# Cumulative sums of the cascade's next segment, issued two interleaving steps later

## The chip, the cores and the metric

The kernel runs on one core of a Trainium2 chip. The metric is the device time of one execution in microseconds (us). Three runs of the kernel before gave 21643.39, 21647.89 and 21668.76 us; the median is 21647.89 us. The engines are called PE (TensorE, matmuls), DVE (VectorE), ACT (ScalarE), POOL (GpSimd) and SP (the queue that issues all DMAs here).

## What is computed

The reference is a network of two layers on x of shape 8 x 128 x 64 x 64. Each layer adds a token mixer and a feed-forward part. The change touches only one part of the second layer's mixer, the *cascade*: two blocks of a Mamba-2 kind in a row, on eight groups of 16 channels, over sequences of 4096 tokens, for each of the 8 images. Cut to what matters, one block is

```
zxbcdt = x @ in_w.T + in_b                     # z, x, B, C, dt
dt  = softplus(dt + dt_bias);  A = -exp(A_log)
xBC = silu(conv3(x, B, C) + conv_b)
Acs  = cumsum(dt * A) within a chunk           # the cumulative sums
Lmat = exp(Acs[l] - Acs[s]) for l >= s
Yd = (C . B) * Lmat @ (x * dt)                 # inside a chunk
states = B * exp(Acs[-1] - Acs) * (x * dt)     # what a chunk adds to the state
Yo = C . state_before * exp(Acs)               # from earlier chunks
y  = (Yd + Yo + D * x) * silu(z);  y = rmsnorm(y) @ out_w.T
```

The state goes from chunk to chunk, so the chunks of one block and one image form a chain. The second block reads the first block's output.

## The kernel before

The 4096 tokens of an image are cut in segments of 256 tokens, 128 segments in all, and each segment in two chunks of 128. Three generators make a segment, and a hand-written loop interleaves them. Each `yield` ends a step.

`ssd_project` (line 942) prepares a segment. It yields after each of two groups of `bc_p` matmuls with their Silu, after `z_p`, after the first `tok_p`, and "silu" after the second `tok_p`, where the activation table for Exp and Ln is loaded (line 321). Its next step (lines 999 to 1007) is softplus: Abs, Exp and Ln on ACT and five small DVE operations, which end in `dA = dt * A`. The next step (line 1008) is `ssd_exponents` (line 914): the matmul `cs_p` makes the cumulative sums of dA, four DVE operations (lines 926 to 929) split them into three bf16 parts `csq`, one DMA writes these to DRAM (line 931), and 16 DMAs load them back as rows (`ssB`, line 936, four; `ssA`, line 939, twelve). The next step (lines 1011 to 1023) makes `dec_p` and its Exp `wd`, multiplied by dt on DVE, and `cd_p` and its Exp `cd`. The last one (lines 1025 to 1034) makes `eA` from the parts with twelve bf16 matmuls. After it, block 0 issues the loads for its next segment (line 1364).

`ssd_chunk` (line 1036) computes one chunk in seven steps:
1. `g_p` (C . B) and its masked copy `gm`; `pad` and `xw` on DVE (x times dt, x times wd); `xD` on POOL.
2. `decays(0)`: four `ss_p` matmuls from `ssA` and `ssB`, and two Exps `E`.
3. `yo_p` from the old state copy `Sd`; `s_p` from `xw`; `masked(0)` (the two E times gm, DVE); the new state `S`, and its copies `Sd` on POOL.
4. `decays(1)`, and the mark "decays".
5. `inside(0)`: `y_p`, the product of E and pad; `yy`; `masked(1)`.
6. `inside(1)`.
7. `yy` plus `y_p`, times silu(z).

`ssd_output` (line 1151) normalizes a segment and projects it with `o_p`.

PSUM has two pools of tiles in the cascade. Tag "a" has two tiles of two banks (`bc_p`, `z_p`, `tok_p`, `g_p`, `ss_p`, `eA_p`, `ms_p`), tag "b" four tiles of one bank (`cs_p`, `dec_p`, `cd_p`, `yo_p`, `s_p`, `y_p`, `o_p`).

The loop at lines 1432 to 1455 takes, for each n, the chunks x[0] (block 0, segment n, first chunk), x[1] (block 1, segment n - 2, first chunk), x[2] (block 0, second chunk) and x[3] (block 1, second chunk). `until(gen, mark, others)` advances gen step by step up to the mark, and after each of its steps advances the first of the others that is not finished by one call. The segment n + 1 of block 0 is prepared beside x[0] up to "silu"; from there the generator is wrapped in `slow`, which gives an empty step ahead of each step's own yield, so that each step takes two calls: the first call after "silu" runs softplus, then come two calls beside the rest of x[1], then four beside x[2] up to "decays", and then `drain` runs all that is left. The segment n - 1 of block 1 is treated in the same way after x[2], beside x[3] and the next x[0]. So `ssd_project` comes twice in a pass of the loop, 256 times in all.

The order of instructions on each engine is not exactly that of the code: Tile orders them when the program is made, from what is ready and from the order in which the code issued them, and gives out the PSUM tiles. Each engine then runs its own list in order, and waits on semaphores. `self.mm`, `self.act`, `self.tt` and the like are helpers, so most instructions of the profile carry the line of a helper (L287, L290, L329, L338) and are told apart by their tiles.

Of the kernel before, what the change touches and what calls it, by code (L numbers as in the profile page):

```python
# [278 lines left out]
class Net:  # L279
# [1054 lines left out]
    def cascade(self, ps):  # L1334

        nc, tc = self.nc, self.tc
        total = self.nb * NSC
        with tc.tile_pool(name="cs", bufs=1) as pl, tc.tile_pool(name="csw", bufs=2) as wk:  # L1340
            ring = self.ssd_rings(pl, CM, SC, 3, 3, 4)
            st = [{"ring": ring, "S": None, "layer": j} for j in range(2)]
            stk, y1, seg = {}, {}, {}

            def place(n):
                return n // NSC, n % NSC

            def load(layer, n):
                if not 0 <= n < total:
                    return  # L1350
                b, k = place(n)
                src = self.xs[b] if layer == 0 else y1[b]
                stk[layer, n] = self.tap_stack(src, k * SC, k == 0, ring)

            def project(layer, n):
                if not 0 <= n < total:
                    return
                t = stk.pop((layer, n))
                for v in self.ssd_project(CM, self.ssw[layer], ring, lambda j: t[:, j, :], SC, wk, ps):
                    if isinstance(v, dict):  # L1360
                        seg[layer, n] = v
                    yield v
                if layer == 0:
                    load(0, n + 1)

            def chunk(layer, n, c):
                if not 0 <= n < total:
                    return
                if c == 0 and n % NSC == 0:
                    st[layer]["S"] = None  # L1370
                yield from self.ssd_chunk(CM, self.ssw[layer], st[layer], seg[layer, n], c, wk, ps)

            def output(layer, n):
                if not 0 <= n < total:
                    return
                b, k = place(n)
                sg = slice(k * SC, (k + 1) * SC)
                for o in self.ssd_output(CM, self.ssw[layer], seg.pop((layer, n)), SC, wk, ps):
                    if o is None:
                        yield  # L1380
                if layer == 0:
                    if k == 0:
                        y1[b] = self.dp.tile([C, L], F32, name="y1", bufs=2)
                    y = wk.tile([C, SC], F32, name="y1s")
                    nc.scalar.copy(y, o)
                    nc.sync.dma_start(y1[b][:, sg], y)
                    load(1, n)
                else:
                    x = wk.tile([C, SC], F32, name="ys")
                    nc.sync.dma_start(x, self.xs[b][:, sg])  # L1390
                    self.stt(x, x, self.w("skip"), o, ALU.mult, ALU.add)
                    nc.vector.tensor_reduce(self.gms[:, b, k : k + 1], x, AX.X, ALU.add)
                    nc.sync.dma_start(self.ys[b][:, sg], x)

            def until(gen, mark, others=()):

                for v in gen:
                    for o in others:
                        if next(o, self) is not self:
                            break  # L1400
                    if v == mark:
                        break

            def between(gen, then):

                yield from gen
                yield next(then, None)

            def both(*gens):

                gens = list(gens)
                while gens:
                    for g in list(gens):
                        if next(g, self) is self:
                            gens.remove(g)
                        yield None

            def drain(*gens):
                for g in gens:
                    for _ in g:  # L1420
                        pass

            def slow(gen):

                for v in gen:
                    yield None
                    yield v

            load(0, 0)
            drain(project(0, 0))  # L1430
            late = p = iter(())
            for n in range(total + 2):
                x = [chunk(0, n, 0), chunk(1, n - 2, 0), chunk(0, n, 1), chunk(1, n - 2, 1)]
                until(x[0], "decays", [p])
                drain(p)
                p = project(0, n + 1)
                rest = between(x[0], x[1])
                until(p, "silu", [rest])
                drain(rest)
                until(x[1], "decays", [late])  # L1440
                p = slow(p)
                next(p, None)
                until(x[1], "end", [p])
                until(x[2], "decays", [p])
                drain(p, late)
                p = project(1, n - 1)
                rest = between(x[2], x[3])
                until(p, "silu", [rest])
                drain(rest)
                first = slow(output(0, n))  # L1450
                until(x[3], "decays", [first])
                p = slow(p)
                next(p, None)
                until(x[3], "end", [p, first])
                late = both(first, slow(output(1, n - 2)))
            drain(late)
# [254 lines left out]
```

## Time and profile before

| What | Value |
|---|---|
| Median of three runs | 21647.89 us |
| The profiled execution | 21652.28 us |
| Its span, first to last instruction | 21650.5 us |
| Mean granted PE clock | 0.930 |
| PE busy | 17287.7 us, 80% |
| DVE busy | 15953.5 us, 74% |
| ACT busy | 11620.6 us, 54% |
| POOL busy | 8896.4 us, 41% |
| `cs_p` of the cascade, first and last start | 11382.2 and 19813.8 us |

A row of the waits view reads: engine and what it was about to run, what it waited for, us in total, times, longest. A row of the timeline reads: start in us, duration in us, engine, line, operation, output <- inputs, shapes, number of instructions merged; in brackets the engine's idle time before it and what ended that. One float32 matmul of the code stands as two instructions, one bf16 matmul as one. Records of a few matmuls can be missing. A row of the windows view gives the busy time of each engine in a stretch, with the number of instructions.

### The profile page before, as it was taken

What the parts mean: (1) busy time and instruction counts of PE and PEld (TensorE: products, weight loads), DVE (VectorE), ACT (ScalarE), POOL (GpSimd) and SP (SyncE); (2) the same over time, 40 slices, a digit from 0 to 9 for tenths busy, and PEclk for the clock granted to TensorE, in tenths of its full rate; (3) what the DMA queues carried; (4) which work ended last, traced back from release to release, by engine and by line L of the source; (5) the groups of instructions that cost most, each with busy time, mean ns of one, the idle gap of its engine ahead of it and who ended that gap; (6) DMA issues with size and microseconds to landing.
All of it is one profiled execution on the core that took longest, in us unless ns stands there. A gap on an engine that the chain in (4) does not pass through costs nothing. (4 is left out here: it accounts for less than half of the span.)

```text
span 21650.5 us, 300665 instructions
## 1 busy us (share of the span) xinstructions
PE 17287.7 (80%) x112733; PEld 8832.8 (41%) x112733; DVE 15953.5 (74%) x21079; ACT 11620.6 (54%) x17646; POOL 8896.4 (41%) x6004
## 2 busy tenths in 40 slices
PE   6777777777777777777778888888888888887999
PEld 2222222222222222225345555555555555554343
DVE  7979798897979889794555666666666666666887
ACT  6555555555555555552535555555555555555442
POOL 6757576675757677573111111111111111112221
PEclk9989899998999999997778999999999999998999
DMA  4534344443434444344420000000000000001110
GB/s 113 130 103 131 103 131 120 115 129 106 129 106 130 111 123 130 106 130 118 137 88 21 25 24 24 24 25 24 24 24 25 24 24 24 24 25 33 39 41 25
DMA packets 804462, 1616.84 MB, mean 75 GB/s; under 512 B 179579, under 2 KB 411931, under 8 KB 802267
## 3 DMA queue, kind: packets, MB, share of 16 engines
q1 hardware_dynamic: 803006, 1597.61, 26.9%
q8 instruction: 891, 14.60, 0.3%
q14 instruction: 565, 4.63, 0.1%
HBM read 1373.56 MB, written 223.74 MB: 74 GB/s over the span
## 5 line engine op out<-in xcount | busy, mean ns | idle before, releaser
L287 PE MATMUL dA<-parts,expand 128*128 128x512 bf16 x12288 | 3448.3, 390 | 2441.5 <-ACT dA L290 1768.8
L329 POOL TENSOR_TENSOR bx<-xE,B 128x1024 f32<-128x1024 f32 x2048 | 4822.2, 2357 | 753.3 <-DVE dA L621 406.9
L290 ACT ACTIVATE dA<-dA,negA 128x512 f32<-128x512 f32 x4096 | 2709.4, 661 | 3726.9 <-PE dA L287 3704.3
L621 DVE TENSOR_TENSOR_SCAN dA<-dA,last,bx 128x1024 f32<-128x1024 f32 x1536 | 3612.2, 2352 | 177.5 <-ACT dA L290 156.7
L287 PEld LDWEIGHTS <-expand 128*128 128x128 bf16 x12288 | 1197.0, 98 | 5226.6 <-issue 4514.1
L338 DVE SCALAR_TENSOR_TENSOR E_cm<-E_cm,gm_cm 128x1024 f32<-128x1024 f32 x2048 | 2444.7, 1235 | 295.0 <-ACT E_cm L290 279.5
L329 DVE TENSOR_TENSOR hc<-dA,C 128x1024 f32<-128x1024 f32 x2048 | 2508.2, 1225 | 166.7 <-DVE dA L621 3.2
L290 ACT ACTIVATE E_cm<-ss_p 128x1024 f32<-128x1024 f32 x2048 | 1998.0, 1023 | 1139.4 <-PE ss_p L287 1134.3
L1129 POOL COPY Sd_cm<-S_cm 64x128 f32<-64x128 f32 x1024 | 785.4, 767 | 3812.3 <-DVE S_cm L329 3699.3
L287 PE MATMUL ss_p<-ssB_cm,ssA_cm 128*128 128x512 bf16 x4096 | 1327.1, 408 | 494.4 <-ACT E_cm L290 407.8
L287 PE MATMUL y_p<-E_cm,pad_cm 128*32 128x128 f32 x32768 | 1457.4, 285 | 47.0 <-DVE E_cm L338 47.0
L621 DVE TENSOR_TENSOR_SCAN dA<-dA,bx 128x1024 f32<-128x1024 f32 x512 | 1174.0, 2293 | 188.5 <-POOL bx L329 128.1
L329 POOL TENSOR_TENSOR xD_cm<-tok_cm,D_cm 128x256 f32<-128x256 f32 x512 | 433.6, 847 | 2001.3 <-PE y_p L287 1206.0
L287 PE MATMUL y<-hc,kt 128*32 128x512 f32 x8192 | 1199.0, 652 | 26.1 <-DVE hc L329 26.1
L287 PEld LDWEIGHTS y_p<-E_cm,pad_cm 128*32 128x32 f32 x32768 | 944.7, 112 | 429.3 <-DVE E_cm L338 158.8
L287 PE MATMUL bc_p<-stk_cm,W_cm 128*128 128x256 f32 x4096 | 1014.4, 391 | 23.9 <-DMA stk_cm<-xs 20.7
L290 ACT ACTIVATE tok_cm<-tok_p 128x384 f32<-128x384 f32 x1024 | 502.9, 491 | 702.7 <-PE tok_p L287 608.6
L329 DVE TENSOR_TENSOR gm_cm<-g_p,kt 128x1024 f32<-128x1024 f32 x512 | 626.0, 1223 | 333.5 <-PE g_p L287 333.3
L338 DVE SCALAR_TENSOR_TENSOR dw<-h,w_second,dw 128x512 f32<-128x512 f32 x1024 | 858.3, 863 | 5.5 <-ACT h L290 1.0
L290 ACT ACTIVATE BC_cm<-bc_p 128x1024 f32<-128x1024 f32 x512 | 524.4, 1024 | 608.7 <-PE bc_p L287 607.2
L287 PE MATMUL tok_p<-W_cm,stk_cm 128*128 128x200 f32 x4096 | 828.2, 345 | 0.1
L287 PEld LDWEIGHTS bc_p<-stk_cm,W_cm 128*128 128x128 f32 x4096 | 750.3, 191 | 189.5 <-issue 94.6
(387 smaller groups left out, 30583.2 us busy)
## 6 DMA issues: line engine op xcount, KB each, us to landing
xE<-dtx_d SPq DMA_DIRECT2D x2048, 512.0 KB
dtx_d<-dtx SPq DMA_DIRECT2D x256, 256.0 KB
x<-x SPq DMA_DIRECT2D x192, 256.0 KB
ssA_cm<-cs_cm SPq DMA_DIRECT2D x3072, 4.0 KB
stk_cm<-xs SPq DMA_DIRECT2D x368, 128.0 KB
stk_cm<-y SPq DMA_DIRECT2D x368, 128.0 KB
x<-in_x_dram SPq DMA_DIRECT2D x64, 256.0 KB
x<-r SPq DMA_DIRECT2D x64, 256.0 KB
```

The lines of the kernel that those rows point to most:

```text
L287: self.ordered(self.nc.tensor.matmul(out, lhsT=lhsT, rhs=rhs, start=start, stop=stop))
L290: i = self.ordered(self.nc.scalar.activation(out, in_, func, **kw))
L329: self.ordered((eng or self.nc.vector).tensor_tensor(out, a, b, op))
L338: self.ordered(self.nc.vector.scalar_tensor_tensor(out=out, in0=a, scalar=s, in1=b, op0=op0, op1=op1))
L621: self.ordered(nc.vector.tensor_tensor_scan(out=t, data0=t, data1=bx.pop(n), initial=0.0 if ch["j"] == 0 else last[:, q : q + 1], op0=ALU. ...
L1129: nc.gpsimd.tensor_copy(Sd[gr, :, g * hi : (g + 1) * hi], S2[gr])
```

## The change

`slow` gets a second argument. The first value of the wrapped generator is preceded by `more` further empty steps; the later ones by one, as before. Both preparations are wrapped with `more = 2`, the outputs as before.

```diff
-            def slow(gen):
+            def slow(gen, more=0):
 
                 for v in gen:
-                    yield None
+                    for _ in range(1 + more):
+                        yield None
+                    more = 0
                     yield v
...
                 until(x[1], "decays", [late])
-                p = slow(p)
+                p = slow(p, 2)
                 next(p, None)
                 until(x[1], "end", [p])
                 until(x[2], "decays", [p])
...
                 until(x[3], "decays", [first])
-                p = slow(p)
+                p = slow(p, 2)
                 next(p, None)
                 until(x[3], "end", [p, first])
```

Softplus is still run by the first call. `ssd_exponents` is run by call 5 in place of 3, the step of dec and cd by call 7 in place of 5, that of eA by call 9 in place of 7, and the loads by call 11 in place of 9. Calls from 8 on are made by the drain.

## The prediction

> **What bounds the kernel now.** I read the page first: the change touches only the cascade, which lies between about 11,400 and 19,840 us, and there TensorE (PE) is the fullest engine. The windows view gives it 7356 of these 8440 us, VectorE (DVE) 5254, ScalarE (ACT) 4721. Then the waits of PE in that stretch, then the timeline at its two largest holes.
>
> ```profile
> engine line waited for: us in total, times, longest us
> PE cs_p L287 <- DVE dA_cm L329: 408.2, 248, 3.8
> PE ss_p L287 <- ACT E_cm L290: 407.1, 508, 1.5
> ...
> PE ss_p L287 <- DMA ssB_cm<-cs_cm: 13.6, 4, 7.6
> ```
>
> So the matmul of the cumulative sums waits for dA, which softplus has just made; the loads of the cs rows make PE wait for almost nothing. One pass of the loop takes 65.0 us (cs_p comes at 14022.33 and again at 14087.28), and 128 segments pass. 408.2 / 128 = 3.19 us of wait per pass. It falls in two places. After layer 1's first chunk (place A):
>
> ```profile
> 14018.21 0.49 PE L287 MATMUL y_p<-kt,xD_cm 128*128 128x128 f32 x2
> 14018.53 0.59 PE L287 MATMUL ss_p<-ssB_cm,ssA_cm 128*128 128x512 bf16 x2
> 14019.51 0.38 PE L287 MATMUL ss_p<-ssB_cm,ssA_cm 128*128 128x512 bf16 x1 [0.38 <-DVE dtr_cm L989]
> 14022.33 0.43 PE L287 MATMUL cs_p<-kt,dA_cm 128*64 128x128 f32 x2 [2.44 <-DVE dA_cm L329]
> 14022.69 0.43 PE L287 MATMUL dec_p<-dA_cm,kt 128*128 128x64 f32 x2
> 14023.06 0.34 PE L287 MATMUL cd_p<-dA_cm,kt 128*64 128x32 f32 x4
> 14023.33 1.03 PE L287 MATMUL ss_p<-ssB_cm,ssA_cm 128*128 128x512 bf16 x2
> 14024.30 1.12 PE L287 MATMUL yo_p<-BC_cm,Sd_cm 128*64 128x128 f32 x6
> ```
>
> and after layer 1's second chunk (place B):
>
> ```profile
> 14063.38 0.43 PE L287 MATMUL cs_p<-kt,dA_cm 128*64 128x128 f32 x2 [0.90 <-DVE dA_cm L329]
> 14063.74 0.93 PE L287 MATMUL g_p<-BC_cm 64*128 64x128 f32 x10
> 14064.60 0.60 PE L287 MATMUL ss_p<-ssB_cm,ssA_cm 128*128 128x512 bf16 x2
> 14065.04 0.33 PE L287 MATMUL dec_p<-dA_cm,kt 128*128 128x64 f32 x2
> 14065.31 0.31 PE L287 MATMUL cd_p<-dA_cm,kt 128*64 128x32 f32 x4
> 14065.44 0.64 PE L287 MATMUL yo_p<-BC_cm,Sd_cm 128*64 128x128 f32 x8
> ```
>
> A waits 2.44 us, B 3.19 - 2.44 = 0.75 on average. After A the windows view shows a further cost (columns: stretch, its us, busy PE, PEld, DVE, ACT, POOL, granted clock, DMA share, GB/s):
>
> ```profile
> 14018.60:14022.30 3.70, 0.91 (x4) 0.13 (x2) 2.06 (x9) 3.53 (x7) 0.50 (x2) 1.00 0.47 145
> 14022.30:14026.80 4.50, 4.47 (x31) 2.53 (x31) 2.36 (x7) 1.23 (x3) 0.00 (x0) 0.62 0.25 67
> 14063.40:14067.50 4.10, 4.10 (x48) 2.97 (x49) 4.03 (x11) 2.38 (x5) 0.00 (x0) 1.00 0.00 2
> ```
>
> PE is busy 0.91 of 3.70 us, and then runs at a mean granted clock of 0.62 for 4.5 us; after B, with the short wait, it stays at 1.00.
>
> **The change part by part.** Counting the calls of the slowed generator: softplus stays at call 1; cumulative sums move from call 3 to 5, dec/cd from 5 to 7, eA from 7 to 9, the next load from 9 to 11. Two calls fall in the old chunk's rest, four in the next chunk up to "decays", the rest in the drain. So cs_p, its four casts and its 17 DMAs are now issued after the next chunk's g_p, gm, pad, xw, xD and first four ss_p; dec_p, cd_p, wd and cd after its yo_p, s_p, first masks, state update, Sd copies and last ss_p. eA and the load are issued directly behind them, past nothing else. Nothing is added or removed, and the softplus chain (table load 1.28 us, then ACT and DVE up to dA) is untouched: what can change is only what PE does while it runs.
>
> Place B. PE now reaches g_p (0.93) and two ss_p (0.60) ahead of cs_p; they ran straight after it without a wait, so they were ready. Together they are longer than the 0.90 us hole: saved 0.75 us per pass. Bounds: 0, if g_p were ready only because cs_p took the time, and 0.90.
>
> Place A. Here the next chunk's g_p cannot fill the hole, since it needs one of the two double banks that ss_p and its Exp hold. But yo_p and s_p of that chunk can. Their operands are old (the state copy Sd ended at 14007.02, xw at 14018.56 at the latest), and yo_p still ran only at 14024.30, about 0.9 us after the Exps that empty dec_p and cd_p at 14023.38 and 14023.64. I read that as a matter of banks: cs_p, dec_p, cd_p, yo_p, s_p and y_p share four single banks and take them in the order in which the code issues them, and y_p holds one. So cs_p, dec_p and cd_p hold the other three while they wait for dA. With dec_p and cd_p issued behind yo_p and s_p, the two get the banks at about 14018.7 and fit in the hole. What that is worth: yo_p 0.64 us (x8, place B) and s_p 0.80 us (16 of them, windows view restricted to s_p, 14063.40 to 14067.90) make 1.44 us of PE work moved out of the path behind cs_p. Bounds: 0, if the banks are not the reason, and 2.44 + 0.38 (the dtr wait before it) if ss_p too fills what is left.
>
> The clock. At 0.62 over 4.5 us PE loses (1 - 0.62) x 4.5 = 1.71 us per pass. If the hole shrinks from 2.44 to 1.0 us, this may go or stay; B's row, at 1.00 after 0.90 us of wait, is the nearer one, A's is the other end. Bounds 0 and 1.71; I take half, 0.85.
>
> The Trainium skill ("TensorE: Matmul & The Clock Gate", HAM oscillation) says that only idle gaps of more than some 3.4 us bring the clock down. A's 2.44 us gap, with 0.62 after it, contradicts that here. By the page this term would be nothing and the time 109 us longer than mine.
>
> What the moves cost. PE: cs, dec, cd are 0.43 + 0.33 + 0.31 us wherever they stand. DVE: the four casts (0.28, 0.28, 0.21, 0.27) fall behind gm (1.23); at B gm already runs between the second and third cast, so the last ends at most 0.5 us later. wd is next read by xw some 5.1 us after it is made at 14001.72 (xw at 14006.79); moving dec_p past yo_p, s_p and two ss_p (0.64 + 0.80 + 0.60) stays inside that cover, and beyond it each us would be a us of xw. SP issues 17 DMAs, the write at 14001.82, the last at 14012.8; the write took 2.70 us to be followed by the first load, so the last rows are there by about 14015.5 (an estimate). Layer 1's ss_p reads them from 14018.53: 3.0 us of cover, against a delay I put at 0.5 to 1.5 us. For A's sums the same reader comes 40 us later. POOL: xD and Sd now stand ahead in issue, but nothing in the moved chain runs there. No wait is added.
>
> What is late next: at A, dA itself at 14022.28. PE gets 1.44 us of work and waits for the rest. Behind it the stretch 14038 to 14053 is PE busy 14.18 of 14.80 us, and 14067.5 to 14083.6 wholly busy, so what PE gains is passed on.
>
> Sum: 1.44 + 0.75 + 0.85 = 3.04 us per pass, x 128 = 389 us. The profiled execution took 21652.28 us (span 21650.5), 4.4 us above the median of 21647.89, so the two can be used alike: 21652 - 389 = **21,263, say 21,260 us**. Without the clock 21,372; with all upper bounds (2.82 + 0.90 + 1.71 = 5.43 us) 20,957.
>
> **The rivals.**
> 1. Only B changes. cs_p at A still goes first because nothing else gets a bank. For it: the order at A held in every pass I looked at. Against: the operands of yo_p were ready. Price: 0.75 x 128 = 96 us, 21,556.
> 2. It does nothing. The order on each engine is set when the program is made, ready work first, and a later issue need not move an instruction that is ready alone; or B's 0.75 is given back as Exp waits of ss_p, which already cost 407.1 / 128 = 3.18 us per pass. 21,650, within 43 us.
> 3. Slower: the rows come late. The sums of B feed, through 17 DMAs, layer 1's ss_p one chunk later. It decides when the casts fall behind more than gm: behind the four masks as well (1.21 each, 4.84) the rows come 1.23 + 4.84 - 3.0 = 3.1 us too late, or the program is ordered so that ss_p stands behind yo_p, cs_p, dec_p and cd_p for the same reason. Less B's 0.75 and A's 1.44 that is 0.9 us, and without A's gain 2.3: 115 to 294 us, middle 205, so 21,857. Against it: the casts are still issued before those masks, and only 13.6 us of waits on these loads are seen now.
>
> **How the numbers follow.** Forecast 0.55 (21,000 to 21,430), rival 1 0.18 (21,430 to 21,605), rival 2 0.11, rival 3 0.16. Forecast and rival 1 are faster by over 0.2% (43 us, about what a measurement of this kernel can tell from no change): 0.73 faster, 0.11 same, 0.16 slower. The range runs from 21,000 (just above the sum of upper bounds, which I give 0.03) to 21,700, so that most of rival 3 and that tail, under 0.2, are left out.
>
> **What would show it.** In the changed trace: at A, yo_p and s_p of the next chunk stand before cs_p, its wait is about 1 us, the clock after it nearer 1.00; at B, g_p and ss_p stand before cs_p and its wait is gone; the passes are 62 us apart. Wrong if cs_p still waits 2.4 us at A (rival 1 or 2), if ss_p at A comes behind cs_p, or waits for ssB or ssA rows by more than 0.5 us per pass (rival 3).

## The result, and the profile after

The changed kernel takes 21954.59 us (median of four runs, 21926.02 to 21963.47), the kernel before 21649.85 us beside it (21643.39 to 21668.76). The ratio is 1.0137, with an interval of 1.0122 to 1.0152: **305 us slower**, where 21,260 us had been forecast. The profiled execution took 21963.47 us, with a span of 21961.5 us and a mean granted clock of 0.911 in place of 0.930.

First, where the time lies. From the first to the last `cs_p` the cascade takes 8728.4 us in place of 8431.6, which is 68.19 in place of 65.87 us for each of 128 passes. These 297 us are nearly the whole difference, which is 311 us between the spans of the two profiled executions (21961.5 and 21650.5). The windows view over the whole cascade (stretch, its us, then busy us of PE, PEld, DVE, ACT and POOL with the number of instructions, clock, DMA share, GB/s), before and then after:

```profile
11400.00:19840.00 8440.00, 7356.18 (x76461) 4992.77 (x76460) 5253.75 (x10174) 4720.63 (x6760) 1534.05 (x1785) 0.95 0.08 24
```

```profile
11400.00:20140.00 8740.00, 7570.53 (x76407) 5152.40 (x76410) 5146.97 (x10168) 4720.56 (x6761) 1150.01 (x1782) 0.90 0.08 23
```

The same work, 76 thousand matmuls, keeps PE busy 214 us longer, while DVE and ACT are not busy longer. PE's idle time grows by only 300 - 214 = 86 us. So most of the loss is not waiting. The matmuls themselves have become longer, and the mean granted clock, 0.90 in place of 0.95, points to the cause.

Now the waits of PE in that stretch (engine and what it was about to run, what it waited for, us in total, times, longest):

```profile
engine line waited for: us in total, times, longest us
PE ss_p L287 <- ACT E_cm L290: 479.7, 647, 1.5
PE cs_p L287 <- DVE dA_cm L329: 437.3, 129, 3.8
...
PE ss_p L287 <- DVE gm_cm L329: 76.3, 104, 0.8
...
PE ss_p L287 <- DMA ssB_cm<-cs_cm: 19.8, 5, 7.5
```

`cs_p` waits about half as often, 129 times in place of 248, but longer in sum, 437 us. The wait at place B is gone and that at place A has grown. PE waits for the rows of `ssB` and `ssA` for 19.8 us in the whole cascade. They are not late for the hole at A either: the last three of their DMAs are issued in the 1.12 us from 14046.30 on, and between 14049 and 14054 no DMA moves anything, while `y_p`, the last matmul ahead of the hole, runs at 14051.44 (windows view: stretch, its us, busy us of PE, PEld, DVE, ACT and POOL, clock, DMA share, GB/s):

```profile
14046.30 1.12 SPq L939 DMA_DIRECT2D ssA_cm<-cs_cm  x3
14049.00:14054.00 5.00, 2.93 (x35) 2.11 (x33) 2.23 (x10) 3.59 (x8) 0.81 (x2) 1.00 0.00 0
```

The timeline of the changed kernel at A:

```profile
14051.44 0.49 PE L287 MATMUL y_p<-kt,xD_cm 128*128 128x128 f32 x2
14055.28 0.44 PE L287 MATMUL cs_p<-kt,dA_cm 128*64 128x128 f32 x1 [3.36 <-DVE dA_cm L329]
...
14055.68 0.90 PE L287 MATMUL yo_p<-BC_cm,Sd_cm 128*64 128x128 f32 x6
...
14056.40 1.20 PE L287 MATMUL s_p<-xw_cm,tok_cm 128*64 128x32 f32 x13
14057.52 1.46 PE L287 MATMUL ss_p<-ssB_cm,ssA_cm 128*128 128x512 bf16 x3
```

Between `y_p` and `cs_p` there is now nothing. The three `ss_p` of x1 that stood there before are behind `cs_p`, `yo_p` and `s_p`, and the hole is 3.36 us in one piece, where it was 0.38 + 2.44. `yo_p` and `s_p` have not moved ahead of `cs_p`. At B the prediction's picture is there, at a small price, a wait of `ss_p` for gm:

```profile
14099.35 0.93 PE L287 MATMUL g_p<-BC_cm 64*128 64x128 f32 x10
14100.21 0.60 PE L287 MATMUL ss_p<-ssB_cm,ssA_cm 128*128 128x512 bf16 x2
14100.75 0.32 PE L287 MATMUL cs_p<-kt,dA_cm 128*64 128x128 f32 x1
...
14102.79 0.59 PE L287 MATMUL ss_p<-ssB_cm,ssA_cm 128*128 128x512 bf16 x2 [0.74 <-DVE gm_cm L329]
```

Last, the clock. The trace records when the granted clock changes (start in us, length in us, share of full speed). Around place A, in the kernel before and then in the changed one:

```
before  14023.192   3.413  0.5        after  14054.374  13.653  0.5
        14026.605  61.440  1.0               14068.027  54.613  1.0
```

All these lengths are multiples of 3.413 us. The clock thus goes by windows of that length, and the useful view is one that cuts the time at their edges. Before, at A:

```profile
14019.78:14023.19 3.41, 0.97 (x9) 0.62 (x8) 1.45 (x7) 2.40 (x6) 0.00 (x0) 1.00 0.71 206
14023.19:14026.60 3.41, 3.41 (x24) 1.75 (x24) 1.81 (x5) 1.01 (x3) 0.00 (x0) 0.50 0.07 17
14026.60:14030.02 3.42, 2.87 (x50) 1.80 (x47) 2.86 (x4) 2.35 (x3) 2.05 (x2) 1.00 0.18 52
```

and after:

```profile
14050.96:14054.37 3.41, 0.97 (x8) 0.39 (x4) 2.04 (x11) 2.91 (x6) 0.81 (x2) 1.00 0.03 12
14054.37:14057.79 3.42, 2.51 (x25) 2.33 (x26) 2.03 (x8) 0.00 (x0) 0.00 (x0) 0.50 0.08 28
14057.79:14061.20 3.41, 3.41 (x14) 1.52 (x12) 1.82 (x4) 1.45 (x3) 1.43 (x2) 0.50 0.37 110
14061.20:14064.61 3.41, 2.87 (x16) 1.02 (x18) 2.34 (x4) 2.68 (x3) 0.26 (x1) 0.50 0.34 70
14064.61:14068.03 3.42, 3.42 (x38) 2.32 (x39) 1.69 (x2) 0.28 (x1) 0.72 (x1) 0.50 0.08 17
14068.03:14071.44 3.41, 2.45 (x42) 1.61 (x41) 1.87 (x3) 0.92 (x1) 0.00 (x0) 1.00 0.27 85
```

In both kernels a window in which PE is busy 0.97 of 3.41 us is followed by one at half speed. Before, that one is busy throughout, and the clock is back after it. After, the hole reaches over the edge of the window and takes 0.91 us of the next one too (`cs_p` comes at 14055.28); later `ss_p` waits 0.54 us for E, and the clock is back only after four windows. PE is at half speed for 1734.5 us of the cascade in place of 884.7, which is 13.55 us per pass in place of 6.91.

### The profile page after: what moved, and what is told of

It is laid out like the page before. It is cut to its first block, busy times and chain, and to the rows that moved or that the text cites. A ratio compares the mean times of both kernels' runs of the same rounds, so it can differ in the third digit from the quotient of the medians.

```text
span 21961.5 us, 300764 instructions
## 1 busy us (share of the span) xinstructions
PE 17517.6 (80%) x112733; PEld 8999.6 (41%) x112733; DVE 15850.8 (72%) x21079; ACT 11623.6 (53%) x17646; POOL 8519.6 (39%) x6004
## 5 line engine op out<-in xcount | busy, mean ns | idle before, releaser
L287 PE MATMUL ss_p<-ssB_cm,ssA_cm 128*128 128x512 bf16 x4096 | 1387.4, 437 | 584.9 <-ACT E_cm L290 479.7
L1129 POOL COPY Sd_cm<-S_cm 64x128 f32<-64x128 f32 x1024 | 457.8, 447 | 3565.4 <-DVE S_cm L329 3456.6
L287 PE MATMUL y_p<-E_cm,pad_cm 128*32 128x128 f32 x32768 | 1575.2, 300 | 4.3 <-DVE E_cm L338 4.2
L329 POOL TENSOR_TENSOR xD_cm<-tok_cm,D_cm 128x256 f32<-128x256 f32 x512 | 379.2, 741 | 2825.8 <-PE y_p L287 2177.8
L287 PEld LDWEIGHTS y_p<-E_cm,pad_cm 128*32 128x32 f32 x32768 | 1004.6, 118 | 496.3 <-issue 181.0
L329 DVE TENSOR_TENSOR yy_cm<-yy_cm,y_p 128x256 f32<-128x256 f32 x496 | 208.2, 420 | 1128.1 <-PE y_p L287 1128.1
```

The source lines that it names most:

```text
L287: self.ordered(self.nc.tensor.matmul(out, lhsT=lhsT, rhs=rhs, start=start, stop=stop))
L329: self.ordered((eng or self.nc.vector).tensor_tensor(out, a, b, op))
L1129: nc.gpsimd.tensor_copy(Sd[gr, :, g * hi : (g + 1) * hi], S2[gr])
```

## The experiments

Two steps had to be explained: why `ss_p` went behind `cs_p`, and where 2.32 us per pass went. The theories:
- **R (rows).** The later sums of layer 1 (moved at B) make the rows that x1's `ss_p` read late in the plan by which Tile orders the program, so `ss_p` is placed behind `cs_p` at A, although on the chip the rows are there.
- **O**, its rival: it is the move at A itself. Later, **D**: it is the later `dec_p` and `cd_p`, or the casts.
- **Clock.** The loss is the half speed behind the longer hole. Its rival, **order**: the loss is that E and what follows come later.

The table holds all kernels. "Steps" are the further empty steps ahead of the sums at A and at B. "Added" are 128 x 128 bf16 matmuls of constants, ahead of x1's first `y_p`, into a half of its bank that `y_p` overwrites. Waits of `cs_p` are medians. Half speed and length are of the cascade, per pass.

| Kernel | Steps A, B | Added | Time, us | Ratio to before, interval | Wait at A | Wait at B | Half speed | Length |
|---|---|---|---|---|---|---|---|---|
| before | 0, 0 | 0 | 21649.85 | 1 | 2.44 | 0.90 | 6.91 | 65.87 |
| after | 2, 2 | 0 | 21954.59 | 1.0137 [1.0122, 1.0152] | 3.36 | 0 | 13.55 | 68.19 |
| e1 | 0, 2 | 0 | 21842.69 | 1.0086 [1.0069, 1.0102] | 3.36 | 0.15 | 9.05 | 67.43 |
| e2 | 2, 0 | 0 | 21712.44 | 1.0026 [1.0017, 1.0035] | 2.43 | 0.90 | 8.56 | 66.38 |
| e3 | 2, 2 | 40 | 21474.02 | 0.9917 [0.9902, 0.9932] | 1.16 | 0.15 | 1.78 | 64.32 |
| e4 | 3, 0 | 0 | 21486.12 | 0.9921 [0.9906, 0.9936] | 1.94 | 0.90 | 6.95 | 64.49 |
| e5 | 2, 0 (dec, cd 2) | 0 | 21652.14 | 0.9997 [0.9987, 1.0007] | 2.43 | 0.90 | 6.98 | 65.69 |
| e6 | 0, 0 | 30 | 21427.78 | 0.9895 [0.9880, 0.9910] | 1.34 | 0.90 | 2.08 | 63.99 |
| e7 | 3, 0 | 30 | 21309.64 | 0.9841 [0.9827, 0.9856] | 0.28 | 0.90 | 1.46 | 63.02 |
| e8 | 2, 2 | 16 | 21643.06 | 0.9996 [0.9987, 1.0005] | 2.50 | 0 | 5.55 | 65.83 |
| e9 | 2, 2, other rows | 0 | 21525.89 | 0.9939 [0.9924, 0.9954] | 0 | 0 | 9.92 | 64.95 |
| e10 | 3, 2 | 30 | 21557.74 | 0.9951 [0.9934, 0.9968] | 0.94 | 0 | 4.60 | 65.13 |

**e1: only B moved.** The first of the two wraps is put back.

```diff
-                p = slow(p, 2)      # layer 0's preparation (A)
+                p = slow(p)
```

> Only the preparation of block 1 (place B) is slowed by two more steps; block 0 (place A) as before. Theory R (the later sums of B put layer 1's ss_p behind cs_p at A, and that makes the hole at A longer): B's wait of 0.75 us goes, A's hole is 3.3 to 3.4 us as in the changed kernel, the time within 60 us of the changed kernel's 21955. Rival O (the harm is done by A's own shift, because yo_p and s_p then lie around cs_p): A keeps 2.44 us, the time is 21650 - 96 = about 21555.

21842.69 us. In the timeline `cs_p` follows on `y_p` directly, as in the changed kernel:

```profile
14026.88 0.49 PE L287 MATMUL y_p<-kt,xD_cm 128*128 128x128 f32 x2
14030.72 0.62 PE L287 MATMUL cs_p<-kt,dA_cm 128*64 128x128 f32 x2 [3.36 <-DVE dA_cm L329]
```

So B's move alone takes `ss_p` out of the hole at A, and by itself makes the kernel slower by 0.86%. O is out as to the order. The time, however, is 112 us under the changed kernel's, and so 52 us below what R gave: the move at A adds something of its own on top.

**e2: only A moved.** The second wrap is put back, the first stays.

```diff
-                p = slow(p, 2)      # layer 1's preparation (B)
+                p = slow(p)
```

> Only the preparation of block 0 (place A) is slowed by two more steps. Theory R: ss_p stays ahead of cs_p at A, the hole stays at 2.44 us, the clock dips for one window of 3.4 us a pass as before, and the time is within 60 us of 21650. Rival O: the hole at A is 3.3 us or more and the time 21950 or above.

21712.44 us, 2 us above R's figure and 54 us above the kernel before that was measured beside it. The wait at A is 2.43 us as before, with `ss_p` ahead of `cs_p`, but half speed has gone from 6.91 to 8.56 us per pass. A's move alone costs 0.26%, and gains nothing: `yo_p` and `s_p` stand behind `cs_p` here too.

**e3: the changed kernel with PE kept busy in the hole.** The lines stand in `ssd_chunk`, behind the one that takes `y_p`; the useful matmuls of that half start over it afterwards.

```diff
         y = ps.tile([128, NH, 128], F32, tag="b", name="y_p")
+        for _ in range(40 if cfg is CM and c == 0 and st["layer"] == 1 else 0):
+            self.mm(y[:, 1], self.spread[:, :128], self.spread[:, :128])
         inside(0)
```

> The changed kernel, with forty bf16 matmuls of 128 columns added ahead of the first y_p of block 1's first chunk, into a half of its bank that is overwritten later; PE's order is otherwise that of the changed kernel, and the added work (about 2.5 us) lies in the hole at A. Clock theory: most of the 305 us is the clock that the hole of 3.36 us brings to one half for 13.65 us a pass; with PE busy in the hole the clock stays at 1.00 there and the time falls to 21400 to 21600. Rival (the order itself costs the time: E, masks and y_p of the chunk come late whatever the clock): 21900 or more, with the clock up.

21474.02 us: 481 us are won by adding 40 x 128 matmuls that do nothing. Around A the windows view shows full speed (hole, and what is behind it):

```profile
14022.50:14026.37 3.87, 2.72 (x43) 2.52 (x43) 2.22 (x10) 2.68 (x6) 0.81 (x2) 1.00 0.10 34
14026.37:14031.00 4.63, 4.03 (x41) 2.59 (x43) 3.32 (x10) 2.11 (x4) 1.59 (x2) 1.00 0.16 46
```

`ss_p` is still behind `cs_p`. The order is thus that of the changed kernel and the time is under that of before. The clock theory holds; "order" alone can't give this. With e6 below, which does the same to the kernel before, it makes a square: without added matmuls the changed kernel is 305 us slower, with them (40 here, 30 in e6) 46 us, 21474.02 against 21427.78. That is hardly clear of the noise: the ratios to before differ by 0.0022, and each has an interval of 0.0015 to both sides. So some 259 of the 305 us go when the hole is filled.

**e4: three steps at A, none at B.** With three, the sums of A are issued behind `yo_p` and `s_p` of x2 and not only behind the four `ss_p` ahead of them.

```diff
-                p = slow(p, 2)      # layer 0
+                p = slow(p, 3)
...
-                p = slow(p, 2)      # layer 1
+                p = slow(p)
```

> Block 0's preparation is slowed by three more steps, block 1's by none. If the four single banks are given out in the order of issue, and cs_p issued ahead of yo_p and s_p is what keeps these two out of the hole, they now run ahead of cs_p, with ss_p: the hole at A falls from 2.44 + 0.38 to 1.0 us or less, the clock stays at 1.00, and the time is 21250 to 21450. If banks are not the reason, PE's order and the hole are those of before and the time is 21650 within 50.

21486.12 us, 0.8% faster than before, but 36 us over the upper end of what was expected, and the hole is 1.94 us, not 1.0. The timeline at A:

```profile
14027.62 0.66 PE L287 MATMUL yo_p<-BC_cm,Sd_cm 128*64 128x128 f32 x8
14028.11 0.61 PE L287 MATMUL s_p<-xw_cm,tok_cm 128*64 128x32 f32 x16
14028.65 0.82 PE L287 MATMUL ss_p<-ssB_cm,ssA_cm 128*128 128x512 bf16 x2
14031.41 0.40 PE L287 MATMUL cs_p<-kt,dA_cm 128*64 128x128 f32 x2 [1.94 <-DVE dA_cm L329]
```

Now `yo_p` and `s_p` are in the hole, as the prediction wanted them. They take 14028.65 - 14027.62 = 1.03 us there and not 1.44, and 0.38 us of that only replaces the earlier wait for dtr: the waiting at A is 2.82 - 1.94 = 0.88 us shorter. The pass is 1.38 us shorter (65.87 - 64.49); where the other 0.5 us come from, no run tells. The half speed behind A stays, 6.95 us per pass.

**e5: as the changed kernel, but the sums of layer 1 at their old place**, with its dec, cd and eA two steps later.

```diff
-            def slow(gen, more=0):
+            def slow(gen, more=0, at=0):
...
-                for v in gen:
-                    for _ in range(1 + more):
+                for k, v in enumerate(gen):
+                    for _ in range(1 + more * (k == at)):
...
-                p = slow(p, 2)      # layer 1
+                p = slow(p, 2, 1)
```

> Both preparations are still wrapped with two more empty steps, but behind layer 1's second chunk (place B) these stand ahead of the step of dec and cd, so that the sums of layer 1 are issued where the kernel before issues them. Theory R (the later sums of layer 1, with their casts and 17 DMAs, are what puts the first ss_p of x1 behind cs_p at place A): the first two ss_p stand ahead of cs_p again, the hole there is about 2.4 us in place of 3.36, PE spends 7 to 9 us of a pass at half clock in place of 13.5, and the time is 21,640 to 21,740. Rival D (it is the later dec and cd, which hold up wd and xw): order, hole and time stay as in the changed kernel, 21,900 to 22,000.

21652.14 us, the time of the kernel before (0.9997, within 0.1%). `ss_p` is back in its place:

```profile
14017.98 0.59 PE L287 MATMUL ss_p<-ssB_cm,ssA_cm 128*128 128x512 bf16 x2
14018.96 0.38 PE L287 MATMUL ss_p<-ssB_cm,ssA_cm 128*128 128x512 bf16 x1 [0.38 <-DVE dtr_cm L989]
14021.77 0.32 PE L287 MATMUL cs_p<-kt,dA_cm 128*64 128x128 f32 x1 [2.43 <-DVE dA_cm L329]
```

As R said, and D falls. Taking back this one step, the sums of layer 1, takes back the whole loss of the changed kernel.

**e9: later sums as in the changed kernel, but x1 reads other rows.** Its `ss_p` take layer 0's rows, loaded long before; the casts and the 17 DMAs are still done. Part of what is computed (x1's decay factors) is changed.

```diff
-                yield from self.ssd_chunk(CM, self.ssw[layer], st[layer], seg[layer, n], c, wk, ps)
+                sg = seg[layer, n]
+                if layer == 1 and c == 0 and (0, n + 2) in seg:
+                    sg["other"] = seg[0, n + 2]
+                yield from self.ssd_chunk(CM, self.ssw[layer], st[layer], sg, c, wk, ps)
...
-                    self.mm(sp[:, g * n : (g + 1) * n], sg["ssA"][:, e, r, :], sg["ssB"][:, e].rearrange("p h l -> p (h l)"))
+                    rows = sg.get("other", sg) if c == 0 else sg
+                    self.mm(sp[:, g * n : (g + 1) * n], rows["ssA"][:, e, r, :], rows["ssB"][:, e].rearrange("p h l -> p (h l)"))
```

> The changed kernel, but the first chunk of each of layer 1's segments (x1) takes its ss_p from the rows of layer 0's current segment, which were loaded long before, in place of those that its own sums make (so x1's decay factors are layer 0's; the casts and all 17 DMAs are still done, and x3 reads its own rows). Theory R (the place of x1's ss_p in PE's list comes from when its rows are due in the plan, since the sums of layer 1 come later): the ss_p of x1, and with them its y_p, stand ahead of cs_p at place A, which fills the hole with the chunk's own work; the wait of cs_p there falls under 1 us, PE at half clock from 13.5 to under 4 us per pass, time 21,250 to 21,550. Rival D (not the rows but the later casts on DVE or the later dec and cd set the order): ss_p stays behind cs_p, 21,900 to 22,000.

21525.89 us, and the hole at A is gone. `ss_p`, `y_p` and `g_p` now run while dA is made, and `cs_p` waits for nothing:

```profile
14037.61 0.59 PE L287 MATMUL ss_p<-ssB_cm,ssA_cm 128*128 128x512 bf16 x2 [0.32 <-ACT E_cm L290]
...
14039.17 1.07 PE L287 MATMUL y_p<-E_cm,pad_cm 128*32 128x128 f32 x28
...
14043.01 0.61 PE L287 MATMUL ss_p<-ssB_cm,ssA_cm 128*128 128x512 bf16 x2
14043.55 0.32 PE L287 MATMUL cs_p<-kt,dA_cm 128*64 128x128 f32 x1
```

Nothing was changed but where x1's `ss_p` read from, so it is the rows that place them, as R said. How Tile weighs them, no run shows. One number missed: half speed is 9.92 us per pass, not under 4. With the order at A, the order elsewhere changed too, and a new hole opened, at `o_p`:

```profile
14053.70 1.12 PE L287 MATMUL o_p<-yz_cm,wo_cm 128*64 128x256 f32 x4 [2.85 <-POOL yz_cm L329]
```

**e6: the order of before, 30 added matmuls.** The lines of e3 with 30 in place of 40, and both wraps as before.

> The kernel before with 30 more 128 x 128 bf16 matmuls (about 1.7 us at full clock) into a half of the bank of x1's first y_p that is overwritten later, ahead of that y_p, in the hole at place A; the order of the rest stays. Clock theory (the hole of 2.44 us brings the clock to half behind it, which costs about 0.32 us for each us at half): PE at half falls from 6.9 to 1 to 2 us per pass, and the time is 21,380 to 21,480. Rival (the clock behind A costs nothing, because what follows waits for DVE and ACT anyway): 21,650 within 43 us, or later by up to 1.7 x 128 = 218 us where the added matmuls stand on the path.

21427.78 us, 1.05% faster than before, with not a useful instruction moved. The hole is 1.34 us, and the clock behind it is 1.00 where it was 0.62:

```profile
14028.90:14033.09 4.19, 2.85 (x38) 2.16 (x36) 2.52 (x12) 3.82 (x7) 0.89 (x2) 1.00 0.33 108
14033.09:14038.00 4.91, 4.68 (x45) 2.69 (x45) 3.73 (x9) 2.82 (x5) 0.79 (x1) 1.00 0.33 86
```

So the kernel before also lost some 227 us to the clock at A.

**e8: the changed kernel with 16 in place of 40 added matmuls.** The same lines as in e3 with another number.

> The changed kernel with 16 in place of 40 added matmuls ahead of x1's first y_p (about 0.9 us at full clock, result overwritten), so that the hole at place A is cut from 3.36 to about 2.45 us, as long as in the kernel before. If the length of the hole sets how long the clock stays at half: 3.4 us per hole as before, 6 to 9 us per pass in all, 21,600 to 21,720. Rival (any hole of over 2 us costs the same, and only the order is paid for): 21,900 to 22,000.

21643.06 us, the time of before. The hole is 2.50 us, and half speed 5.55 us per pass. Two fifths of the dose do 311 of the 481 us. Among e3, e8 and the changed kernel, which have the same order at A, the time follows half speed. The order still costs a little: e8 takes as long as the kernel before with 1.36 us less at half speed.

**e7: both gains together.** Three steps at A, none at B (e4), with 30 added matmuls (e6).

> Layer 0's preparation with three more empty steps, layer 1's with none, and the 30 added matmuls ahead of x1's first y_p (their result is overwritten). If the hole's length and the clock behind it are two costs that add: the 21,486 us of the same kernel without the added matmuls less what the clock gives (6.95 us at half per pass down to about 1, times 0.32 us, times 128 = 240 us): 21,220 to 21,300. Rival (one gives back the other: with the yo_p and s_p in the hole there is no room, and the added matmuls push the path): 21,450 to 21,600.

21309.64 us, 1.6% faster than before and the fastest of all; 10 us over the range. `cs_p` waits 0.28 us at A, and 141.3 us in all:

```profile
PE ss_p L287 <- ACT E_cm L290: 477.9, 633, 1.5
PE cs_p L287 <- DVE dA_cm L329: 141.3, 243, 3.4
```

**e10: e7 with B moved too**, by two steps as in the changed kernel.

> As the fastest so far (layer 0's preparation with three more empty steps, 30 added matmuls ahead of x1's first y_p, whose result is overwritten, 21,310 us), but layer 1's preparation with two more empty steps as in the changed kernel. If what the later sums of layer 1 cost is the clock (hidden here) and ss_p's place costs little: place B's 0.9 us is saved, 21,200 to 21,300. If ss_p's place behind cs_p costs by itself, because E comes later and y_p and the masks with it: 21,330 to 21,450.

21557.74 us, 248 us slower than e7, and outside both ranges. The wait at B is gone, but `ss_p` is behind `cs_p` at A again, and its waits for E have grown from 477.9 to 565.8 us:

```profile
PE ss_p L287 <- ACT E_cm L290: 565.8, 758, 1.5
PE cs_p L287 <- DVE dA_cm L329: 138.7, 130, 4.5
```

Half speed is 4.60 us per pass in place of 1.46. Both terms are there: by the size found below, 3.14 us at half cost 1.0 of the 2.11 us per pass, and about 1.1 us are left for the order.

**The size of the clock term.** Three pairs have the same order, but for single matmuls, and differ in the added ones. A us of half speed costs, in cascade length: after to e3 (68.19 - 64.32) / (13.55 - 1.78) = 0.33 us, before to e6 1.88 / 4.83 = 0.39, e4 to e7 1.47 / 5.49 = 0.27. The changed kernel has 6.64 us more at half than before, which by these costs 1.8 to 2.6 us, 2.2 in the middle, of the 2.32 us. The square of e3 and e6 gives 259 / 128 = 2.0 us. So the clock is most of the loss. The rest is small and goes both ways: the longer hole at A (3.36 - 2.82 = 0.54 us more), the waits of `ss_p` for gm (76.3 us in place of 9.3, 0.52 us more per pass) and for E (479.7 in place of 407.1, 0.57 more), against the gain at B (0.75 us).

The share of the order is not the same in every kernel. By the same costs it is about 1.1 us per pass in e10 against e7, and in e1 it is the larger one: e1 has 2.14 us more at half speed than before, which cost 0.6 to 0.8 us, but its pass is 1.56 us longer. Why the order costs less in the changed kernel than in e1 and e10 stays open.

## Why the prediction was wrong, point by point

Two steps failed. The move at B was put down as a gain of 0.75 us per pass, 96 us, with "No wait is added", though it moves `ss_p` behind `cs_p` at A and alone costs 184 us (e1, 21842.69 against 21658.48). And the move at A was to bring `yo_p` and `s_p` into the hole, which it does not. So the hole grew from 2.82 to 3.36 us in place of shrinking, and the clock term changed its sign.

- **What bounds the kernel**: right. PE bounds the cascade, its two holes are the waits for dA, and the clock behind A matters. e6 and e3 show that it mattered more than anything else in the sum.
- **Place B, 0.75 us**: right as a mechanism. `g_p` and `ss_p` go first and the wait is gone. 0.74 us comes back on many passes as a wait of the next `ss_p` for gm (76.3 us in all, 0.60 us per pass, where it was 9.3 us in all), much as rival 2 had it for Exp.
- **Place A, 1.44 us**: this step failed. It rested on the sentence that `yo_p` and `s_p` "get the banks at about 14018.7" once `dec_p` and `cd_p` are issued behind them. They don't: in the changed kernel and in e2 both stand behind `cs_p`. They go first only in e4, where `cs_p` too is issued behind them. The banks that `dec_p` and `cd_p` held were not what kept them back, or not alone; whether it was `cs_p`'s own bank or its place in the order of issue, no run tells apart. Where the step does happen (e4) it is worth 1.03 us of work in the hole, not 1.44, though the whole pass is 1.38 us shorter.
- **The clock, 0.85 us gained**: right in what it is about, wrong in sign. It was bounded by 0 and 1.71 us, as if it could only get better, since the hole was to shrink. The hole grew, and the clock cost about 2 us (2.2 by the pairs, 2.0 by the square).
- **The cost of the moves**: "3.0 us of cover, against a delay I put at 0.5 to 1.5 us" was right for the chip, where the rows are not waited for (19.8 us in all), and beside the point. The cover had to hold in the plan that sets the order (e9). This is the second half of rival 3 as it stood ("the program is ordered so that ss_p stands behind yo_p, cs_p, dec_p and cd_p"), with a chance of 0.16 and a price of 115 to 294 us. It came with 305, and by a different sum: the price was to be rows that come 3.1 us too late, less the gains at B and A, and was for the most part the clock. In fact `ss_p` stands behind `cs_p`, `yo_p` and most of `s_p`, and ahead of `dec_p`.
- **The range** ended at 21,700 and left most of rival 3 out. The price given there had no clock term, although the same text had a row with 0.62 behind a hole of 2.44 us, so that any longer hole had to cost more.
- **The rule of the Trainium skill** ("TensorE: Matmul & The Clock Gate", HAM oscillation), that there should be no idle gaps of over some 3.4 us, was rightly put second to the row. The same page, in "What's actually happening", states a free-running window of 3413 ns, and the lengths of 3.413 us in the trace agree with that. By the windows above a gap of 2.44 us is enough where it lies in one window, since it leaves PE 0.97 us of work there.

## What to carry to other kernels

Before a producer is issued later, ask which reader's place in the program depends on it, and not only whether the data will be there in time: a reader that is planned late is late, even if the chip has its data 2 us before, as here. A hole in front of the engine that bounds the kernel costs more than its length where the clock answers to it; cut the profile at the edges of the clock's windows and see how busy each is. Work that does nothing can be a cheap test of this: 40 added matmuls in the hole told most of the clock's share from the order's in one run.

## What was not expected of the hardware

Cut at the edges of the windows, the cascade shows how the clock goes with PE's busy share, and that this share alone does not decide. In the kernel before the clock fell behind 170 windows that were busy 0.17 to 0.63 of the time (median 0.29), in the changed one behind 168, none over 0.58. It stayed full behind none under 0.47 in these two. But in the kernel before it also stayed full behind 210 windows that were busy between 0.47 and 0.58, such as the first of these two:

```profile
14033.43:14036.85 3.42, 1.63 (x7) 0.48 (x5) 2.83 (x3) 2.59 (x3) 0.00 (x0) 1.00 0.03 8
14036.85:14040.26 3.41, 3.00 (x23) 2.58 (x23) 2.98 (x3) 2.75 (x5) 0.00 (x0) 1.00 0.00 0
```

The clock came back only behind windows that were busy nearly from end to end (0.95 and more before, 0.88 and more after). That is not enough either: of the 335 windows behind which the changed kernel stayed at half, 109 were busy 0.95 and more, and of 84 in the kernel before, 58 were. The window 14057.79 to 14061.20 shown above is one of them, busy 3.41 of 3.41 us with 14 matmuls. What is counted beside the busy time of the records stays open.

So a long hole at full speed brings half speed, and a short wait at half speed may keep it there: in the window 14061.20 to 14064.61 of the changed kernel there is a wait of 0.54 us for E, at 14062.82. This fits the four windows after against the usual one before; no run varied it by itself. Open too is how the falls depend on where a hole lies in the window: e8, with a hole of 2.50 us as long as that of before, had no half speed at all in some passes and four windows in others.
